# Scan step: the exponent of a power split over two exponentials, log(1 - e) ahead of sg, and seven unread products a step

## The chip, the cores and the metric

The kernel runs on one core of a Trainium2 chip. The metric is the time on the device in microseconds (us). The engines named below work side by side and meet through semaphores: TensorE (PE, matrix products; PEld are its weight loads), VectorE (DVE, elementwise work and reductions), ScalarE (ACT, functions such as exp and log), GpSimd (POOL) and SyncE (SP, which here issues transfers).

## The reference, cut to what matters

The program is a stack of six sublayers over a state of 2 x 2048 tokens with 256 channels. The change touches only the first one, a recurrent scan over 2048 steps. Its state h holds, for each of 2 batches, 256 channels and 16 modes, a complex number (two floats). One step is:

```
h_carrier = h.mean(axis=1)                      # over the 256 channels
T     = cos((phase(xr_t) - phase(h_carrier)) / 2) ** 2
alpha = exp(dt_t * A_neg)
expo  = 1 + (1 - alpha) * 0.5 * (1 - T)
cmag  = min(exp(expo * log(mag(h) + 1e-8)), 10)
h = from_polar(cmag, phase(h)) + B_t * (dt_t * x_t)
h = from_polar(tanh(mag(h)), phase(h))
y_t = sum(C_t * h)
```

Each step needs the h of the step before, and the mean over the channels couples all of them.

## The kernel before, in words

**Layout.** The 2 batches, 16 modes and 4 groups of channels make 128 rows (partitions); the 64 channels of a group lie along the free axis (J = 64). So nearly every operation of a step works on a tile of 128 x 64 floats, and the two parts of a complex number are two such tiles (`p[:, 0]`, `p[:, 1]`).

**Loops.** A hardware loop runs 4 turns of 512 steps; in a turn the steps are unrolled as 32 groups of 16. `step` writes one step. The order of the instructions on each engine is the order in which they are written (`manual_schedule`), each engine runs its own in order, and a semaphore holds an instruction until what it reads is there.

**A step.** hs holds each row's sum of h over its 64 channels, made by the reduction that also writes the new h (hist, L479).

1. PE multiplies hs with a fixed matrix (L408), eight small products into hc and hd, which sum the four groups of channels: the carrier. It then makes the output products of the step before (yps, L490).
2. ACT takes the log of x (lh, L412), squares and sums hc (sq, L416), and gets the inverse length of the carrier by a log and an exponential (L425, ci L426). VectorE forms the dot product of carrier and input direction (dot, L418).
3. The power's exponent less 1, applied to the log of the squared magnitude, is (alpha - 1)/8 times the carrier's cosine less 1. VectorE makes kd and lg, the log of the squared magnitude (L422, L423), and gl = lg times the decay ng (L435). ACT makes ek = exp(kd) (L427), c1 = ci times dot minus 1 (L428, named c in the trace: trailing digits of names are left out there) and fac = exp(c1 times gl) (L440).
4. VectorE multiplies h with ek (L437, L438), then with fac (L443), adds the input bx (L445), and forms the squared magnitudes m2 and r1 (L447 to L454). While it does, ACT prepares the next step's bx (L389) and, in some steps, decays of the next group.
5. ACT takes logs and exponentials: lm, lr, m, ir, e = exp(-2m), rm, le = log(1 + e) (L468, in the trace under m, whose buffer it uses), sg = exp(-le) (L469), then lb, k1, k2c (L471 to L473). tanh(m) is (1 - e) times sg.
6. VectorE multiplies p with ir (L475), with e - 1 (L477), and with -sg in the reduction that writes hist and hs (L479). Behind it stand x, dl and kc for the next step (L483 to L485).

A small product of ci (L431) writes one element of hd; it makes PE wait for ACT and VectorE at that point.

## Time and profile before

| what | us |
|---|---|
| median of 3 runs | 14357.04 (14350.03 to 14368.9) |
| the profiled execution | 14364.49 |
| its span, first to last instruction | 14362.8 |
| busy in the span: DVE, ACT, PE | 9934.6, 9106.3, 5808.5 |
| mean duration of sg, fac, c, lh | 0.223, 0.348, 0.285, 0.256 |
| mean duration of a product into hc, into hd | 0.203, 0.193 |

A line of the timeline gives the start, the duration, the engine, the line of the kernel, the operation, what it writes and reads, its shape and how many instructions it merges; in square brackets stands how long the engine had been idle and what released it. PEclk is TensorE's granted clock as a share of full speed; in the row of slices it is in tenths. Two instructions of one engine overlap in part, so that the spacing of their starts is shorter than a duration.

### The profile page before, as it was taken

To read this page: it belongs to the slowest core of one execution; us is meant where nothing else is said; L and a number is where in the kernel's file an instruction comes from. 1 tells how busy PE (TensorE), PEld (TensorE's weight loads), DVE (VectorE), ACT (ScalarE), POOL (GpSimd) and SP (SyncE) were. 2 spreads that over 40 slices of the span, in tenths; PEclk is the share of its full clock that TensorE was granted. 3 is DMA by queue.
4 is the path that set the end of the run, shared out by engine and by line. 5 is a ranking of instruction groups with operands and counts; after the bars stand their busy time and mean duration, and the time that the engine had idled before them with its cause. 6 is when DMAs were issued, how large, how long until landed. Compare 5 with 4: busy or idle time off the path is not lost. (4 is left out here: it accounts for less than half of the span.)

```text
span 14362.8 us, 279683 instructions
## 1 busy us (share of the span) xinstructions
PE 5808.5 (40%) x76520; PEld 3905.5 (27%) x76520; DVE 9934.6 (69%) x61067; ACT 9106.3 (63%) x46835; POOL 418.8 (3%) x496
## 2 busy tenths in 40 slices
PE   4222222222222222222222222222598665978889
PEld 1111111111111111111111111111355444544445
DVE  6888888788888878888887888888566211455552
ACT  3777877777777777777777777777454100134442
POOL 0000000000000000000000000000000000121110
PEclk6555555555555555555555555555598787989999
DMA  3000000000000000000000000000000677132210
GB/s 78 13 16 15 15 16 16 14 16 16 13 16 16 13 16 16 13 16 16 13 16 16 13 16 16 13 16 16 13 4 14 170 186 174 39 79 35 34 28 14
DMA packets 349068, 460.94 MB, mean 32 GB/s; under 512 B 204930, under 2 KB 244937, under 8 KB 346452
## 3 DMA queue, kind: packets, MB, share of 16 engines
q1 hardware_dynamic: 296276, 319.90, 9.8%
q10 hardware_dynamic: 36352, 88.61, 2.6%
q0 software_dynamic: 14848, 34.36, 0.8%
q8 instruction: 612, 10.03, 0.3%
q14 instruction: 980, 8.03, 0.2%
HBM read 385.55 MB, written 52.46 MB: 30 GB/s over the span
## 5 line engine op out<-in xcount | busy, mean ns | idle before, releaser
L408 PE MATMUL hc<-hs,mean 128*32 128x2 f32 x16384 | 586.3, 203 | 7250.6 <-DVE hs L479 7186.2
L408 PEld LDWEIGHTS hc<-hs,mean 128*32 128x32 f32 x16384 | 410.5, 140 | 7462.8 <-DVE hs L479 7398.0
L475 DVE TENSOR_TENSOR p<-p,ir 128x64 f32<-128x64 f32 x4096 | 739.5, 222 | 1062.4 <-ACT ir L464 1062.4
L490 PE MATMUL yps<-cs,hist 128*64 128x8 f32 x8192 | 1225.0, 259 | 13.4 <-DVE hs L479 13.4
L460 ACT ACTIVATE lm<-m 128x64 f32<-128x64 f32 x2048 | 466.2, 228 | 1179.7 <-DVE m L452 1179.7
L389 ACT ACTIVATE bx<-dx,tc 128x64 f32<-128x64 f32 x4098 | 1169.7, 332 | 0.0
L1519 ACT ACTIVATE d_p<-ps_e 128x512 f32<-128x512 f32 (+3 forms) x1280 | 599.4, 537 | 755.9 <-PE ps_o L1500 537.2
L490 PEld LDWEIGHTS yps<-cs,hist 128*64 128x64 f32 x8192 | 1033.2, 218 | 45.4 <-DVE hs L479 13.8
L443 DVE TENSOR_TENSOR p<-p,fac 128x64 f32<-128x64 f32 x4096 | 739.4, 222 | 421.6 <-ACT fac L440 421.6
L412 ACT ACTIVATE lh<-x 128x64 f32<-128x64 f32 x2048 | 525.2, 256 | 551.1 <-DVE x L483 551.0
L479 DVE CUSTOM_DVE_ANT_0 hist<-p,sg 128x64 f32<-128x64 f32 x4096 | 764.0, 223 | 23.5 <-ACT lb L471 5.1
L440 ACT ACTIVATE fac<-gl,c 128x64 f32<-128x64 f32 x2048 | 712.3, 348 | 68.9 <-DVE p L437 3.0
L477 DVE SCALAR_TENSOR_TENSOR p<-e,p 128x64 f32<-128x64 f32 x4096 | 738.8, 222 | 11.8 <-ACT sg L469 10.5
L445 DVE TENSOR_TENSOR p<-p,bx 128x64 f32<-128x64 f32 x4096 | 723.9, 218 | 0.0
L428 ACT ACTIVATE c<-ci,dot 128x1 f32<-128x1 f32 x2048 | 584.2, 285 | 0.0
L1512 PE MATMUL ps_e<-d_qt,d_kt 128*128 128x512 f32 (+3 forms) x1280 | 556.7, 444 | 43.9 <-ACT d_p L1519 35.5
L1166 PE MATMUL ps_c<-toep,c_x 64*32 64x128 f32 x18432 | 386.0, 321 | 383.8 <-issue 382.7
L1469 PE MATMUL ps_m<-d_kt,d_qt 128*128 128x512 f32 (+3 forms) x1280 | 501.3, 438 | 97.4 <-DVE d_part L1474 37.6
L408 PE MATMUL hd<-hs,mean 128*32 128x2 f32 x16384 | 539.7, 193 | 0.0
L431 PE MATMUL hd<-ident,ci 128*1 128x1 f32 x4096 | 386.9, 164 | 358.8 <-ACT ci L426 358.8
L1479 DVE TENSOR_REDUCE d_part<-ps_m 128x1 f32<-128x512 f32 x768 | 494.7, 683 | 41.7 <-PE ps_m L1469 41.1
L437 DVE SCALAR_TENSOR_TENSOR p<-hist,ek 128x64 f32<-128x64 f32 x2048 | 460.8, 225 | 84.5 <-ACT ek L427 0.9
(441 smaller groups left out, 21583.2 us busy)
## 6 DMA issues: line engine op xcount, KB each, us to landing
toep<-in_C_krev ACTq DMA_DIRECT2D x64, 1216.0 KB, 14.4
toep<-in_C_krev SPq DMA_DIRECT2D x64, 1216.0 KB, 10.1
ng<-dtd SPq DMA_DIRECT2D x258, 256.0 KB, 3.5
dx<-dxd SPq DMA_DIRECT2D x258, 256.0 KB, 4.1
d_kt<-d_kd SPq DMA_DIRECT2D x128, 128.0 KB, 4.3
d_qt<-d_qd SPq DMA_DIRECT2D x128, 128.0 KB, 4.2
y<-ys SPq DMA_DIRECT2D x512, 8.0 KB, 1.9
c_xd<-c_xs POOLq DMA_DIRECT2D x32, 256.0 KB, 6.7
```

The source lines that it names most:

```text
L389: A.activation(bx[o][:, k2], tg[j][2][:, k], AF.Identity, scale=tg[j][0][:, k2, k : k + 1], bias=0.0 if k2 else SMALL,)
L408: nc.tensor.matmul(out[r : r + 32], mean[:, r : r + 32], hs[i], start=True, stop=True)
L428: A.activation(c1, ci, AF.Identity, scale=dot, bias=-1.0)
L440: A.activation(fac, gl, AF.Exp, scale=c1)
L443: V.tensor_tensor(p[:, k2], p[:, k2], fac, ALU.mult)
L445: V.tensor_tensor(p[:, k2], p[:, k2], bx[o][:, k2], ALU.add)
L475: V.tensor_tensor(p[:, k2], p[:, k2], ir, ALU.mult)
L477: V.scalar_tensor_tensor(p[:, k2], e, -1.0, p[:, k2], ALU.add, ALU.mult)
L479: V.tensor_tensor_reduce(out=hn[:, k2], in0=p[:, k2], in1=sg, scale=-1.0, scalar=0.0 if k2 else J * SMALL, op0=ALU.mult, op1=ALU.add, accu ...
L490: nc.tensor.matmul(yps[:, k, :], hist[g][:, k, k2], tg[g][3][:, k2, k], start=k2 == 0, stop=k2 == 1)
L1512: nc.tensor.matmul(s[:, q0:], ks[kt // 4][:, hh, kt % 4 * P : (kt % 4 + 1) * P], q[:, hh, q0:], start=True, stop=not diag,)
L1519: A.activation(pr[:, q0:], s[:, q0:], AF.Exp, scale=0.25)
```

## The change

**The exponent.** With L = lg and gl = L times ng, the old step formed exp(kd) times exp(gl (ci dot - 1)). The new one forms ex = kd - gl and ngd = gl times dot on VectorE, then ea = exp(ex) and fac = exp(ci times ngd) on ACT. c1 is gone.

**Where the logs come from.** x and its log lh are gone. A new log ld = log(1 - e) is taken on ACT right after le and ahead of sg; th = ld - le is the log of the tanh. lg and kd are now made at the end of a step, behind the reduction, from th, kc and dl, and gl at the head of the next, ahead of the dot product. dl is made from p ahead of the reduction, no longer from hist behind it.

**Buffers.** lb uses the buffer of lr in PSUM; its own is gone.

**Seven products.** After the product of ci, PE makes seven products of a 128 x 128 by a 128 x 512 tile of ones in bf16 into a PSUM tile named idle, which nothing reads.

In the setup the same start values are formed with other names, and one tile of ones is written. The core of the diff:

```diff
--- before.py
+++ after.py
@@ -329,7 +329,7 @@
 
             hist = [new(cp, [P, TG, 2, J], f"hist{j}") for j in range(2)]
             hs = [new(cp, [P, 2], f"hs{j}") for j in range(2)]
-            x, kc, dl = ([new(cp, [P, J], f"{n}{j}") for j in range(2)] for n in ("x", "kc", "dl"))
+            lg, kd = ([new(cp, [P, J], f"{n}{j}") for j in range(2)] for n in ("lg", "kd"))
             bx = [new(cp, [P, 2, J], f"bx{j}") for j in range(2)]
             tg = [[new(cp, sh, f"{n}{j}") for n, sh in (
                 ("tc", [P, 6, TG]), ("ng", [P, TG, J]), ("dx", [P, TG, J]),
...
@@ -392,6 +391,8 @@
                 )
 
             hc, hd = new(pp, [P, 2], "hc"), new(pp, [P, 2], "hd")
+            warm, idle = cp.tile([P, 512], BF16, name="warm", tag="warm"), new(pp, [P, 512], "idle")
+            V.memset(warm, 1.0)
             w = lambda sh, name: new(wp, [P, *sh], name)
             wa = lambda name: new(pa, [P, J], name)
 
@@ -408,8 +409,8 @@
                         nc.tensor.matmul(out[r : r + 32], mean[:, r : r + 32], hs[i], start=True, stop=True)
                 before()
 
-                lh, lg, kd = (w([J], n) for n in ("lh", "lg", "kd"))
-                A.activation(lh, x[i], AF.Ln, scale=-1.0)
+                gl, ex, ea, ngd = (w([J], n) for n in ("gl", "ex", "ea", "ngd"))
+                V.tensor_tensor(gl, lg[i], ng, ALU.mult)
 
 
                 sq, n2c = w([2], "sq"), w([1], "n2c")
@@ -419,25 +420,25 @@
                     out=junk, in0=hd, in1=tc_[:, 4:6, k], scale=1.0, scalar=0.0, op0=ALU.mult, op1=ALU.add,
                     accum_out=dot,
                 )
-                V.scalar_tensor_tensor(kd, kc[i], 0.5, dl[i], ALU.mult, ALU.add)
-                V.scalar_tensor_tensor(lg, lh, 2.0, kc[i], ALU.mult, ALU.add)
-                ln, ci, c1, ek = wa("lr")[:, 0:1], w([1], "ci"), w([1], "c1"), w([J], "ek")
+                V.tensor_tensor(ex, kd[i], gl, ALU.subtract)
+                V.tensor_scalar(ngd, gl, dot, None, ALU.mult)
+                ln, ci = wa("lr")[:, 0:1], w([1], "ci")
                 A.activation(ln, n2c, AF.Ln, bias=1e-18)
                 A.activation(ci, ln, AF.Exp, scale=-0.5)
-                A.activation(ek, kd, AF.Exp)
-                A.activation(c1, ci, AF.Identity, scale=dot, bias=-1.0)
+                A.activation(ea, ex, AF.Exp)
 
 
                 nc.tensor.matmul(hd[32:33, 0:1], ci, self.ident[:, 0:1], start=True, stop=True)
 
-
-                gl = w([J], "gl")
-                V.tensor_tensor(gl, lg, ng, ALU.mult)
+                for _ in range(7):
+                    nc.tensor.matmul(idle, warm[:, 0:P], warm, start=True, stop=True)
+
+
                 p = w([2, J], "p")
-                V.scalar_tensor_tensor(p[:, 0], h[:, 0], SMALL, ek, ALU.add, ALU.mult)
-                V.tensor_tensor(p[:, 1], h[:, 1], ek, ALU.mult)
+                V.scalar_tensor_tensor(p[:, 0], h[:, 0], SMALL, ea, ALU.add, ALU.mult)
+                V.tensor_tensor(p[:, 1], h[:, 1], ea, ALU.mult)
                 fac = w([J], "fac")
-                A.activation(fac, gl, AF.Exp, scale=c1)
+                A.activation(fac, ngd, AF.Exp, scale=ci)
                 act_gap(k)
                 for k2 in range(2):
                     V.tensor_tensor(p[:, k2], p[:, k2], fac, ALU.mult)
@@ -460,14 +461,15 @@
                 A.activation(lm, m2, AF.Ln)
                 A.activation(lr, r1, AF.Ln)
                 A.activation(m, lm, AF.Exp, scale=0.5)
-                ir, e, sg, rm = (w([J], n) for n in ("ir", "e", "sg", "rm"))
+                ir, e, sg, rm, ld = (w([J], n) for n in ("ir", "e", "sg", "rm", "ld"))
                 A.activation(ir, lr, AF.Exp, scale=-0.5)
                 A.activation(e, m, AF.Exp, scale=-2.0)
                 A.activation(rm, lm, AF.Exp, scale=-1.0)
                 le = wa("m")
                 A.activation(le, e, AF.Ln, bias=1.0)
+                A.activation(ld, e, AF.Ln, scale=-1.0, bias=1.0)
                 A.activation(sg, le, AF.Exp, scale=-1.0)
-                lb, k1, k2c = wa("lb"), w([J], "k1"), w([J], "k2c")
+                lb, k1, k2c = wa("lr"), w([J], "k1"), w([J], "k2c")
                 A.activation(lb, m2, AF.Ln, bias=MAG_EPS)
                 A.activation(k1, rm, AF.Ln, scale=MAG_EPS, bias=1.0)
                 A.activation(k2c, lb, AF.Exp, scale=-0.5)
@@ -475,14 +477,18 @@
                     V.tensor_tensor(p[:, k2], p[:, k2], ir, ALU.mult)
                 for k2 in range(2):
                     V.scalar_tensor_tensor(p[:, k2], e, -1.0, p[:, k2], ALU.add, ALU.mult)
+                th, kc, dl = (w([J], n) for n in ("th", "kc", "dl"))
+
+                V.scalar_tensor_tensor(dl, p[:, 0], 0.5 * SMALL, rm, ALU.mult, ALU.mult)
                 for k2 in range(2):
                     V.tensor_tensor_reduce(
                         out=hn[:, k2], in0=p[:, k2], in1=sg, scale=-1.0, scalar=0.0 if k2 else J * SMALL,
                         op0=ALU.mult, op1=ALU.add, accum_out=hs[o][:, k2 : k2 + 1],
                     )
-                V.scalar_tensor_tensor(x[o], e, -1.0, sg, ALU.add, ALU.mult)
-                V.scalar_tensor_tensor(dl[o], hn[:, 0], -SMALL, rm, ALU.mult, ALU.mult)
-                V.scalar_tensor_tensor(kc[o], k2c, 2.0 * MAG_EPS, k1, ALU.mult, ALU.add)
+                V.tensor_tensor(th, ld, le, ALU.subtract)
+                V.scalar_tensor_tensor(kc, k2c, 2.0 * MAG_EPS, k1, ALU.mult, ALU.add)
+                V.scalar_tensor_tensor(lg[o], th, 2.0, kc, ALU.mult, ALU.add)
+                V.scalar_tensor_tensor(kd[o], kc, 0.5, dl, ALU.mult, ALU.add)
 
             def project(g, k, yps):
 
```

More of the change, by code (lines that the diff above doesn't have):

```diff
@@ L341, in scan @@
             V.tensor_scalar(hs[1][:, 0:1], hs[1][:, 0:1], J * SMALL, None, ALU.add)
-            n0 = new(wp, [P, J], "lh")
+            n0, n1, n2h = (new(wp, [P, J], n) for n in ("kc", "dl", "th"))
             A.preload_act_table_set(LOG_EXP)
             V.tensor_tensor(n0, first[:, 1], first[:, 1], ALU.mult)
-            V.tensor_tensor(kc[1], first[:, 0], first[:, 0], ALU.mult)
-            V.tensor_tensor(n0, n0, kc[1], ALU.add)
-            A.activation(kc[1], n0, AF.Ln, bias=MAG_EPS)
-            A.activation(x[1], kc[1], AF.Exp, scale=-0.5)
-            V.scalar_tensor_tensor(kc[1], x[1], 2.0 * MAG_EPS, kc[1], ALU.mult, ALU.add)
-            A.activation(n0, n0, AF.Ln)
-            V.tensor_tensor(kc[1], kc[1], n0, ALU.subtract)
-            A.activation(x[1], n0, AF.Exp, scale=-1.0)
-            V.scalar_tensor_tensor(dl[1], first[:, 0], -SMALL, x[1], ALU.mult, ALU.mult)
-            A.activation(x[1], n0, AF.Exp, scale=0.5)
-            V.tensor_scalar(x[1], x[1], -1.0, None, ALU.mult)
+            V.tensor_tensor(n1, first[:, 0], first[:, 0], ALU.mult)
+            V.tensor_tensor(n0, n0, n1, ALU.add)
+            A.activation(lg[1], n0, AF.Ln, bias=MAG_EPS)
+            A.activation(n1, lg[1], AF.Exp, scale=-0.5)
+            V.scalar_tensor_tensor(lg[1], n1, 2.0 * MAG_EPS, lg[1], ALU.mult, ALU.add)
+            A.activation(n0, n0, AF.Ln)
+            V.tensor_tensor(n2h, lg[1], n0, ALU.subtract)
+            A.activation(n1, n0, AF.Exp, scale=-1.0)
+            V.scalar_tensor_tensor(n1, first[:, 0], -SMALL, n1, ALU.mult, ALU.mult)
+            V.scalar_tensor_tensor(kd[1], n2h, 0.5, n1, ALU.mult, ALU.add)
             yv = y.rearrange("p k (b t) -> p k b t", b=B)
```

## The prediction

> **What bounds the kernel now.** I read the slices of the span first. Twenty-eight of forty look alike, with the TensorE clock at 0.5: this is the recurrent scan, 2048 steps one after another.

> ```profile
> span 14362.8 us, 279683 instructions
> DVE  6888888788888878888887888888566211455552
> ACT  3777877777777777777777777777454100134442
> PEclk6555555555555555555555555555598787989999
> ```

> No engine is full in these slices, so the bound is a chain that runs through all the engines. Between 1000.4 and 10183.9 us lie 1915 steps, so a step takes 4.797 us on average and the 2048 take 9824 us, 68% of the span. Next I laid 80 steps of the timeline (5000 to 5400 us) over each other: 71 of them last 4.76 or 4.77 us (4.765 below), the offsets inside agree within 0.01 us, and a few steps are 0.12 to 0.35 us longer. One such step, start first, then duration:

> ```profile
> 5004.30 0.22 DVE L483 SCALAR_TENSOR_TENSOR x<-e,sg 128x64 f32<-128x64 f32 x1
> 5004.44 0.29 PE L408 MATMUL hc<-hs,mean 128*32 128x2 f32 x8 [3.83 <-DVE hs L479]
> 5004.80 0.17 ACT L416 ACTIVATE sq<-hc 128x2 f32<-128x2 f32 x1
> 5004.90 0.16 DVE L418 CUSTOM_DVE_ANT_0 junk<-hd,tc 128x2 f32<-128x2 f32 x1
> 5005.13 0.22 DVE L423 SCALAR_TENSOR_TENSOR lg<-lh,kc 128x64 f32<-128x64 f32 x1
> 5005.30 0.17 ACT L426 ACTIVATE ci<-lr 128x1 f32<-128x1 f32 x1
> 5005.38 0.22 DVE L435 TENSOR_TENSOR gl<-lg,ng 128x64 f32<-128x64 f32 x1
> 5005.51 0.28 ACT L428 ACTIVATE c<-ci,dot 128x1 f32<-128x1 f32 x1
> 5005.83 0.35 ACT L440 ACTIVATE fac<-gl,c 128x64 f32<-128x64 f32 x1
> 5006.21 0.36 DVE L443 TENSOR_TENSOR p<-p,fac 128x64 f32<-128x64 f32 x2 [0.20 <-ACT fac L440]
> 5008.07 0.36 DVE L475 TENSOR_TENSOR p<-p,ir 128x64 f32<-128x64 f32 x2 [0.56 <-ACT ir L464]
> 5008.19 0.23 ACT L468 ACTIVATE m<-e 128x64 f32<-128x64 f32 x1
> 5008.40 0.36 DVE L477 SCALAR_TENSOR_TENSOR p<-e,p 128x64 f32<-128x64 f32 x2
> 5008.45 0.22 ACT L469 ACTIVATE sg<-m 128x64 f32<-128x64 f32 x1
> 5008.77 0.23 DVE L479 CUSTOM_DVE_ANT_0 hist<-p,sg 128x64 f32<-128x64 f32 x1
> ```

> Take T as the start of x (5004.30). The reader should see one ring: the sums hs, the mean products on PE (T+0.14), sq, ci (T+1.00), c, fac (T+1.52), then VectorE's p times fac (T+1.90), a middle part, and hist (T+4.47), which is 0.30 before the next T. Gaps tell where time goes: c takes 0.28 and fac waits for it.

> **Spacings used**, all from these steps. Independent VectorE operations start 0.14 apart. A dependent one starts 0.26 after its source (lg to gl). ACT to VectorE or back costs 0.03 after the end (ek ends T+1.31, p starts T+1.34). An operation that waits for two engines starts 0.19 after its predecessor in a pair, 0.33 after the pair's first (L475 to L477). A reduction starts about 0.15 after an ordinary operation: in the attention stage at 13641.24 and 13641.85 it follows a reduce 0.61 later, where two reduces stand 0.595 apart. Logarithm to the next ACT operation: 0.15 (k1 to k2c).

> **Part 1, the first half of a step (T to p times fac).** Removed are lh (0.26 on ACT, beside PE's work, so worth nothing: sq starts 0.07 after PE is done with hc) and c (0.28, on the path). What takes c's place as the last thing is VectorE's new chain, which now precedes the exponentials. In the order in which the changed kernel issues it:
> - th T+0, kc T+0.14, lg (needs kc) T+0.40, kd T+0.54, gl (needs lg) T+0.67, the dot product T+0.82 with its accumulator read T+0.91;
> - ex (needs gl) T+0.93, ngd (needs dot) T+1.07, ended T+1.29;
> - ea on ACT at ex's end: 0.93 + 0.22 + 0.03 = T+1.18, ended T+1.43 (0.25, as ek);
> - the pair p from ea T+1.46 and T+1.60, and p times fac, a two-engine wait on that pair, at 1.46 + 0.33 = T+1.79;
> - fac itself: not before ea + 0.15 = T+1.33, nor before ngd's end with about 0.03 to 0.11 for its two waits, T+1.32 to T+1.40; with 0.35 + 0.03 it releases VectorE at T+1.71 to T+1.78, just earlier.

> So p times fac moves from T+1.90 to T+1.79: **-0.11 us a step**. The bounds are -0.16 (fewer wait penalties) and -0.05 (fac's waits cost more).

> **Part 2, the second half.** Two operations enter ahead of hist. ld, a logarithm, goes on ACT behind le: before, sg waited 0.26 after le began, for its result, and ld takes 0.15 of that. sg then starts at 3.88 + 0.15 + 0.15 = T+4.18 rather than 4.14, and is ready at T+4.43. On VectorE dl stands behind the L477 pair (T+4.10, 4.24). It waits for both engines, so it starts at 4.10 + 0.33 = T+4.43. hist follows at 4.43 + 0.15 = T+4.58 instead of 4.47: **+0.11 us a step**. Bounds: +0.04 if dl starts 0.14 after its pair and hist 0.14 after dl, +0.19 if hist keeps the 0.23 distance it has now from the operation ahead of it. sg, ready 0.15 before, hides ld; without that cover ld would cost up to 0.15. lb, k1 and k2c slip by 0.04; k2c is ready near T+4.85, kc asks for it at 4.58 + 0.30 + 0.14 = T+5.02. lb's move into lr's buffer adds no wait: users of both run in order on ACT.

> [...] le, with that bias, lasts 0.23 and k1 0.25, and k2c starts 0.15 after k1. I take the rows.

> **Part 3, seven products.** bf16 128x128 by 128x512, behind the ci product (T+1.22 to 1.41). No such product is in the trace. The nearest row is a 512-column product of attention at the slow clock: L1469 at 13389.17, the next at 13389.60, so 0.43 each with its weight load hidden. 7 x 0.43 = 3.0: they end near T+4.45 and PE is next wanted at T+4.77+0.14. They cost nothing; the cover is 0.4 us a step. At 0.53 each (a 0.10 load, as of L983's bf16 weights, exposed) they would end at T+5.1 and delay the sums by 0.2.

> Do they raise the clock, and does that help? [...] after 10300 us, 1189 consecutive stretches of 3.413 us each show a clock of exactly 0.5 or 1. For instance (span, PE busy, PE weight loads, VectorE, ACT, POOL, clock):

> ```profile
> 11235.57:11238.99 3.41, 3.41 (x128) 3.00 (x114) 0.00 (x0) 0.00 (x0) 0.00 (x0) 0.50 0.59 149
> 11238.99:11242.40 3.41, 2.24 (x98) 1.94 (x101) 0.66 (x2) 1.07 (x2) 0.00 (x0) 1.00 0.12 25
> 11245.81:11249.23 3.41, 0.24 (x18) 0.00 (x0) 0.00 (x0) 0.00 (x0) 0.00 (x0) 1.00 1.07 260
> 11249.23:11252.64 3.41, 0.47 (x23) 0.47 (x30) 0.00 (x0) 0.00 (x0) 0.00 (x0) 0.50 1.09 258
> ```

> A full stretch is followed by clock 1, a stretch that is 7% busy by 0.5. All 104 rises follow at least 0.76 busy; most of 103 falls less than 0.4. The new step has PE busy some 90% while slow and 55% when fast, so the clock should go up and fall back at times: a mean of 0.6 to 0.95, I take 0.8. [...] By the rows they release nothing: at the slow clock ci would already let fac start at T+1.21 and dot's input is there at T+0.60, while VectorE asks for them at T+1.33 and T+0.82. So 0, with -0.02 a step as the other end.

> **Sum.** -0.11 + 0.11 + 0 = 0.00 us a step, with ends of about -0.12 and +0.14 if all lean one way. Two more VectorE operations a step lengthen the occasional long steps (0.03 a step now) by 2/26, +0.002, 5 us in all; the setup's changed lines are a handful of operations. Against the profiled execution (span 14362.8, 14364.5 in all) that gives 14370; the median of the runs is 7.4 lower, so 14362 on its scale.

> **Rivals.**
> - *Slower, by dl ahead of hist* (36%). hist is held 0.165 to 0.19 rather than 0.11 if the reduction again keeps the 0.23 after the operation ahead of it. It decides once hist stands 0.14 or more after its old offset with the first half as forecast; at 0.19 the step loses 0.08, +164 us: 14526. For it: hist stands 0.23 behind L477 today. Against: there hist itself has two waits, after the change one.
> - *Faster* (29%). dl doesn't wait its second wait out, hist moves only 0.04: net -0.07, -143 us: 14219. Or the faster clock counts because VectorE's chain is quicker than summed. Against: the L475 to L477 pair has exactly dl's form and shows 0.33.
> - *Products in the way* (inside the slower case, 3%): above 0.5 us each they push the mean products; at 0.53 and a slow clock +0.2 x 2048 = +410 us. For it: the weights are loaded seven times. Against: the 0.43 row.
> - *The products don't lift the clock*: PEclk stays 0.5 in the scan, time as forecast, since PE isn't on the path either way.

> **How the numbers follow.** Two tenths of a percent (29 us, 0.014 a step) is about what a measurement of this kernel can tell from no change. No change within it: 35%, the likeliest, 14362, own range 14333 to 14391. Faster 29%, slower 36%. Halving the ends of the rivals gives roughly -0.05 and +0.055 a step as what leaves out a tenth on each side: 14255 to 14475.

> **What would show it.** p times fac at T+1.79 (right if 1.75 to 1.83), ea starting at T+1.18 on ex, hist at T+4.58 with dl 0.15 ahead, sg not the last to arrive; period 4.75 to 4.79. Wrong if fac is released by ci (then PE counts), if mean products wait for PE's queue, or if hist starts with sg's end.

## The result and the profile after

The changed kernel takes 14329.0 us (median of 20 runs) where the kernel before takes 14351.7 us in the same runs: ratio 0.9985, 95% interval 0.9979 to 0.9991. That is 22.7 us less, 0.15%: inside the band of 0.2% that the prediction called no change, but with 20 runs a side it is resolved. It is a small gain where exactly none was forecast. The profiled execution of the changed kernel was the longest of its 20 (14342.7 us, span 14341.0).

The page of the changed kernel, its head and slices:

```profile
span 14341.0 us, 310403 instructions
...
DVE  6888888888888888888888888888576111455552
ACT  3777777777777777777777777777354000134442
...
PEclk6777776777777777777777777777698787989999
```

The scan still fills the same slices and neither VectorE nor ACT is full. TensorE's clock in the scan went from 0.50 to 0.72 on average; the time barely moved. Whether the faster clock bought any of the small gain, the first experiment tests.

One step from the timeline (start, duration, engine, line); T is the start of th:

```profile
5051.51 0.22 DVE L488 TENSOR_TENSOR th<-ld,m 128x64 f32<-128x64 f32 x1
5051.65 0.29 PE L409 MATMUL hc<-hs,mean 128*32 128x2 f32 x8 [0.95 <-DVE hs L484]
5051.90 0.22 DVE L490 SCALAR_TENSOR_TENSOR lg<-th,kc 128x64 f32<-128x64 f32 x1
5052.00 0.17 ACT L417 ACTIVATE sq<-hc 128x2 f32<-128x2 f32 x1 [0.55 <-PE hc L409]
5052.18 0.22 DVE L413 TENSOR_TENSOR gl<-lg,ng 128x64 f32<-128x64 f32 x1
5052.43 0.23 DVE L423 TENSOR_TENSOR ex<-kd,gl 128x64 f32<-128x64 f32 x1
5052.50 0.17 ACT L427 ACTIVATE ci<-lr 128x1 f32<-128x1 f32 x1
5052.69 0.26 ACT L428 ACTIVATE ea<-ex 128x64 f32<-128x64 f32 x1
5052.85 2.96 PE L434 MATMUL idle<-warm 128*128 128x512 bf16 x7
5052.91 0.35 ACT L441 ACTIVATE fac<-ngd,ci 128x64 f32<-128x64 f32 x1
5052.98 0.23 DVE L438 SCALAR_TENSOR_TENSOR p<-hist,ea 128x64 f32<-128x64 f32 x1 [0.16 <-ACT ea L428]
5053.31 0.36 DVE L444 TENSOR_TENSOR p<-p,fac 128x64 f32<-128x64 f32 x2
5055.45 0.24 ACT L470 ACTIVATE ld<-e 128x64 f32<-128x64 f32 x1
5055.50 0.36 DVE L479 SCALAR_TENSOR_TENSOR p<-e,p 128x64 f32<-128x64 f32 x2
5055.59 0.20 ACT L471 ACTIVATE sg<-m 128x64 f32<-128x64 f32 x1
5055.83 0.23 DVE L482 SCALAR_TENSOR_TENSOR dl<-p,rm 128x64 f32<-128x64 f32 x1
5055.97 0.22 DVE L484 CUSTOM_DVE_ANT_0 hist<-p,sg 128x64 f32<-128x64 f32 x1
```

ea starts as soon as ex is there (T+1.18), 0.02 after ci has ended, and p times fac starts at T+1.80 behind the pair p. The rows of the two pages for p times fac, before and after, show the same: VectorE's idle time ahead of it, 421.6 us that ended with fac, has shrunk to 9.8 us.

```profile
L443 DVE TENSOR_TENSOR p<-p,fac 128x64 f32<-128x64 f32 x4096 | 739.4, 222 | 421.6 <-ACT fac L440 421.6
L444 DVE TENSOR_TENSOR p<-p,fac 128x64 f32<-128x64 f32 x4096 | 741.3, 222 | 9.8 <-DVE p L444 6.2
```

In the second half sg has ended at 5055.79, 0.18 before hist starts: hist stands behind dl. The timeline prints hundredths of a microsecond, which is too coarse here; the records of the trace have nanoseconds. With the short steps between 5000 and 5400 us laid over each other (72 before, 69 after), the offsets are these (medians, in us). sq stands at 0.49 in the step shown, whose mean products are slow (0.29), and at 0.447 in most.

| from T, us | before | forecast | after |
|---|---|---|---|
| sq | 0.495 | 0.49 | 0.447 |
| ea | (ek 1.062) | 1.18 | 1.171 |
| fac | 1.526 | 1.33 to 1.40 | 1.398 |
| p times fac | 1.906 | 1.79 | 1.789 |
| from p times fac to the e - 1 pair | 2.194 | as before | 2.194 |
| from that pair to hist | 0.369 | 0.48 | 0.471 |
| from hist to the next T | 0.297 | 0.30 | 0.290 |
| a short step | 4.766 | 4.765 | 4.744 |

So 0.117 us is gained in the first half, 0.102 is lost between the pair and hist, and 0.007 is gained behind hist. The net -0.022 is worth -45 us over 2048 steps. Part is given back by steps that are longer than the short ones: over the scan, with the gaps of some 12 us between the four turns of the loop left out, they add 39 us before and 52 us after, 0.019 and 0.026 us a step. With the gaps 2 us shorter this gives -45 + 13 - 2 = -34 us, and in the two profiled executions the scan, from the first T to the last, is indeed 33.7 us shorter (9819.6 to 9785.9).

These two executions as a whole differ by 21.8 us only, since the rest of the program, nearly all of it behind the scan, took 11.9 us longer. The change does not touch the program behind the scan, and there the ten traces of this case range from 4159 to 4184 us. Whether the change has a share in these 12 us, one trace a kernel can't say.

### The profile page after: what moved, and what is told of

Read it like the earlier page. It is cut to its first block, busy times and chain, and to the rows that moved or that the text cites. A ratio compares the mean times of both kernels' runs of the same rounds, so it can differ in the third digit from the quotient of the medians.

```text
span 14341.0 us, 310403 instructions
## 1 busy us (share of the span) xinstructions
PE 10559.7 (74%) x90856; PEld 5123.5 (36%) x90856; DVE 10322.3 (72%) x65164; ACT 8537.4 (60%) x44786; POOL 419.0 (3%) x496
## 5 line engine op out<-in xcount | busy, mean ns | idle before, releaser
L434 PE MATMUL idle<-warm 128*128 128x512 bf16 x14336 | 5241.6, 528 | 0.0
L434 PEld LDWEIGHTS <-warm 128*128 128x128 bf16 x14336 | 1567.3, 121 | 2187.0 <-issue 1601.2
L409 PE MATMUL hc<-hs,mean 128*32 128x2 f32 x16384 | 533.0, 190 | 2182.5 <-DVE hs L484 2117.9
L409 PEld LDWEIGHTS hc<-hs,mean 128*32 128x32 f32 x16384 | 356.8, 120 | 3741.8 <-DVE hs L484 3676.7
L477 DVE TENSOR_TENSOR p<-p,ir 128x64 f32<-128x64 f32 x4096 | 738.0, 221 | 1062.4 <-ACT ir L465 1062.4
L417 ACT ACTIVATE sq<-hc 128x2 f32<-128x2 f32 x2048 | 352.4, 172 | 1107.9 <-PE hd L409 672.4
L496 PE MATMUL yps<-cs,hist 128*64 128x8 f32 x8192 | 969.4, 227 | 2.5 <-DVE hs L484 2.5
L496 PEld LDWEIGHTS yps<-cs,hist 128*64 128x64 f32 x8192 | 780.5, 167 | 38.2 <-DVE hs L484 5.7
L479 DVE SCALAR_TENSOR_TENSOR p<-e,p 128x64 f32<-128x64 f32 x4096 | 739.8, 221 | 5.4 <-DVE p L479 4.1
L441 ACT ACTIVATE fac<-ngd,ci 128x64 f32<-128x64 f32 x2048 | 712.2, 348 | 1.0 <-DVE p L438 1.0
L438 DVE SCALAR_TENSOR_TENSOR p<-hist,ea 128x64 f32<-128x64 f32 x2048 | 460.1, 225 | 322.5 <-ACT ea L428 322.4
L428 ACT ACTIVATE ea<-ex 128x64 f32<-128x64 f32 x2048 | 524.3, 256 | 81.0 <-DVE ex L423 4.9
```

Source lines behind the costliest of these rows:

```text
L409: nc.tensor.matmul(out[r : r + 32], mean[:, r : r + 32], hs[i], start=True, stop=True)
L434: nc.tensor.matmul(idle, warm[:, 0:P], warm, start=True, stop=True)
L441: A.activation(fac, ngd, AF.Exp, scale=ci)
L477: V.tensor_tensor(p[:, k2], p[:, k2], ir, ALU.mult)
L479: V.scalar_tensor_tensor(p[:, k2], e, -1.0, p[:, k2], ALU.add, ALU.mult)
L496: nc.tensor.matmul(yps[:, k, :], hist[g][:, k, k2], tg[g][3][:, k2, k], start=k2 == 0, stop=k2 == 1)
```

## The experiments

The theory: the first half is held by VectorE's chain kc, lg, gl, ex, then ea and p, so that PE's clock releases nothing; the second half is held by dl alone, and ld hides behind the wait of sg. The rivals: the clock is what brought the gain, and ld holds hist. Ratios are to the kernel before, with 95% intervals.

### The changed kernel without the seven products

```diff
-                for _ in range(7):
-                    nc.tensor.matmul(idle, warm[:, 0:P], warm, start=True, stop=True)
```

> The changed kernel without the seven unread products; everything else as in it. Theory (VectorE's chain kc, lg, gl, ex, ea, p holds the first half, so the products release nothing): the clock falls back to 0.50 in the scan, sq starts 0.04 us later than in the changed kernel (T+0.49 instead of T+0.45), p times fac stays at T+1.79, the short step stays at 4.74 us; the long steps may get fewer[...]: 14329 or up to 15 us less. Rival (the faster clock is what made the changed kernel's step 0.02 us shorter): the step grows by 0.02 to 0.04 us, 14370 to 14410.

Measured: 14342.2 us, ratio 0.9987 (0.9981 to 0.9994). Both kernels took some 10 us more in these runs than in those of the result (before 14361.9), so the ratios are what can be compared. The clock is back at 0.5. One step:

```profile
5052.69 0.22 DVE L484 TENSOR_TENSOR th<-ld,m 128x64 f32<-128x64 f32 x1
5053.18 0.17 ACT L415 ACTIVATE sq<-hc 128x2 f32<-128x2 f32 x1 [0.55 <-PE hc L407]
5054.48 0.36 DVE L440 TENSOR_TENSOR p<-p,fac 128x64 f32<-128x64 f32 x2
```

sq is back at T+0.49, and p times fac stays at T+1.79; the short step is 4.747 against 4.744, where the rival asked for 0.02 to 0.04 more. The ratio is within 0.0002 of that of the full change (0.9985), with intervals of 0.0006 to each side: if the products give or cost anything in this kernel, it is not more than about 12 us (an estimate from the two intervals). Their absence did not take the long steps away (they add 58 us in the scan, against 52 with the products), so the products are not what makes them, which I had thought possible.

### The seven products alone, in the kernel before

```diff
+                for _ in range(7):
+                    nc.tensor.matmul(idle, warm[:, 0:P], warm, start=True, stop=True)
...
-                lb, k1, k2c = wa("lb"), w([J], "k1"), w([J], "k2c")
+                lb, k1, k2c = wa("lr"), w([J], "k1"), w([J], "k2c")
```

> The kernel before with the seven products alone (lb shares lr's buffer, as in the change, to make room). In this kernel sq, ci, c and fac are the ring, so a PE that is done earlier should count: sq moves from T+0.49 to T+0.45 on average at a clock near 0.77, p times fac from T+1.90 to T+1.86, the step from 4.765 to 4.725 us: -82 us, less some 15 us for more long steps, so about 14285. Rival (PE is off the path here as well, or the products cost as much as they give): within 0.2% of before.

Measured: 14310.5 us, 0.9961 (0.9947 to 0.9975): -51 us. The sign is as the theory has it, the size smaller. The reason is in the timeline of this kernel:

```profile
5044.43 0.22 DVE L488 SCALAR_TENSOR_TENSOR x<-e,sg 128x64 f32<-128x64 f32 x1
5044.57 0.24 PE L410 MATMUL hc<-hs,mean 128*32 128x2 f32 x8 [1.88 <-DVE hs L484]
5046.30 0.36 DVE L448 TENSOR_TENSOR p<-p,fac 128x64 f32<-128x64 f32 x2 [0.21 <-ACT fac L445]
5049.15 0.22 DVE L488 SCALAR_TENSOR_TENSOR x<-e,sg 128x64 f32<-128x64 f32 x1
5049.29 0.28 PE L410 MATMUL hc<-hs,mean 128*32 128x2 f32 x8 [0.85 <-DVE hs L484]
5051.06 0.36 DVE L448 TENSOR_TENSOR p<-p,fac 128x64 f32<-128x64 f32 x2 [0.20 <-ACT fac L445]
5053.92 0.22 DVE L488 SCALAR_TENSOR_TENSOR x<-e,sg 128x64 f32<-128x64 f32 x1
```

The two steps are of two kinds. In the first the eight products into hc take 0.24, p times fac starts 1.87 after x, and the step lasts 4.72. In the second they take 0.28, it starts at 1.91, and the step lasts 4.77, as in the kernel before; so lb's shared buffer, which this run has as well, costs nothing. A fast clock at the mean products is worth 0.043 us a step, and over the scan 1142 of 1894 short steps have it: 0.043 x 0.60 x 2048 = 53 us. I had reckoned as if every step gained. The same products that buy 51 us in the kernel before buy nothing that could be measured in the changed one: the change took PE off the ring.

### dl moved out of the way of the reduction

```diff
-                V.scalar_tensor_tensor(dl, p[:, 0], 0.5 * SMALL, rm, ALU.mult, ALU.mult)
...
                 V.scalar_tensor_tensor(kc, k2c, 2.0 * MAG_EPS, k1, ALU.mult, ALU.add)
+                V.scalar_tensor_tensor(dl, p[:, 0], 0.5 * SMALL, rm, ALU.mult, ALU.mult)
                 V.scalar_tensor_tensor(lg[o], th, 2.0, kc, ALU.mult, ALU.add)
```

> The changed kernel with dl moved from ahead of the reduction into the gap between kc and lg, where lg waits for kc anyway. Theory (dl is all that holds hist up): hist stands 0.37 us behind the first e - 1 product again instead of 0.47, T+4.35 for T+4.45, the step falls by 0.10 to 4.64 us, -205 us: about 14125. Rival (ld ahead of sg holds hist as much as dl does): hist waits for sg, which is ready at T+4.31, with its two waits at T+4.39 to 4.42: the step falls by 0.03 to 0.06 only, 14205 to 14270.

Measured: 14173.3 us, 0.9864 (0.9849 to 0.9879), -189 us to before. Its timeline, VectorE and sg of one step:

```profile
5056.50 0.36 DVE L479 SCALAR_TENSOR_TENSOR p<-e,p 128x64 f32<-128x64 f32 x2
5056.60 0.20 ACT L471 ACTIVATE sg<-m 128x64 f32<-128x64 f32 x1
5056.87 0.23 DVE L483 CUSTOM_DVE_ANT_0 hist<-p,sg 128x64 f32<-128x64 f32 x1
...
5057.30 0.22 DVE L488 SCALAR_TENSOR_TENSOR kc<-k2c,k 128x64 f32<-128x64 f32 x1
5057.44 0.22 DVE L489 SCALAR_TENSOR_TENSOR dl<-p,rm 128x64 f32<-128x64 f32 x1
5057.57 0.22 DVE L490 SCALAR_TENSOR_TENSOR lg<-th,kc 128x64 f32<-128x64 f32 x1
```

hist stands 0.37 behind the pair's first again, as in the kernel before, where the changed kernel has 0.47. By the rival it would be 0.41 to 0.44. The step is 4.667, not 4.64. lg now starts 0.270 after kc where it had 0.251, which puts p times fac at T+1.805 instead of 1.789, so dl is not wholly free in the gap; and what was gained behind hist, 0.007, is gone again.

### dl moved, and no products

> The changed kernel with dl between kc and lg and without the seven products. By the theory that the products release nothing: the same short step as with dl moved and the products kept, and up to 15 us less for fewer long steps. By the rival that the clock counts: 0.02 to 0.04 us a step, 40 to 80 us, more than with the products.

Measured: 14173.4 us, 0.9868 (0.9853 to 0.9883), at a clock of 0.5 in the scan. It equals the run above; with and without products the mean step between 1000 and 4000 us is 4.707 us. This is the simplest of the kernels here that beat both, by 188 us to before.

### ld behind sg

```diff
                 A.activation(le, e, AF.Ln, bias=1.0)
-                A.activation(ld, e, AF.Ln, scale=-1.0, bias=1.0)
                 A.activation(sg, le, AF.Exp, scale=-1.0)
+                A.activation(ld, e, AF.Ln, scale=-1.0, bias=1.0)
```

> The changed kernel with ld behind sg instead of ahead of it; dl stays ahead of the reduction. Theory (sg isn't what hist waits for, dl is): sg starts 0.04 us earlier, T+4.04, and hist stays at T+4.45; step 4.74 us, 14340 on the scale where before has 14362, that is the changed kernel's own time within 15 us. Rival (ld ahead of sg costs its 0.15): hist earlier by up to 0.15, the step 4.60 to 4.70, 80 us or more off.

Measured: 14344.6 us, 0.9984 (0.9977 to 0.9990). The two ends of one step:

```profile
5053.15 0.22 DVE L488 TENSOR_TENSOR th<-ld,m 128x64 f32<-128x64 f32 x1
...
5057.18 0.23 ACT L470 ACTIVATE sg<-m 128x64 f32<-128x64 f32 x1
5057.47 0.23 DVE L482 SCALAR_TENSOR_TENSOR dl<-p,rm 128x64 f32<-128x64 f32 x1
5057.61 0.22 DVE L484 CUSTOM_DVE_ANT_0 hist<-p,sg 128x64 f32<-128x64 f32 x1
```

sg starts at T+4.03 instead of 4.08, hist stays at T+4.46. ld ahead of sg costs nothing as long as dl stands where it does.

### Both behind

> The changed kernel with dl between kc and lg and ld behind sg. Theory: hist is set by the 0.37 us behind the first e - 1 product, not by sg, so no gain over dl alone moved (4.67 us, 14173); and ld in the way of k2c may make kc late: k2c is then ready near T+4.80, kc asks for it at T+4.67 + 0.13 = 4.80, so 0 to +0.05 us a step, 14173 to 14275. Rival (sg holds hist once dl is out of the way): hist 0.04 earlier, 14090.

Measured: 14277.3 us, 0.9937 (0.9923 to 0.9950): 90 us less than before, where dl alone moved gave 189 less, so about 100 us of that is lost, at the unfavourable end of the theory. One step:

```profile
5051.01 0.36 DVE L479 SCALAR_TENSOR_TENSOR p<-e,p 128x64 f32<-128x64 f32 x2
5051.06 0.23 ACT L470 ACTIVATE sg<-m 128x64 f32<-128x64 f32 x1
5051.38 0.23 DVE L483 CUSTOM_DVE_ANT_0 hist<-p,sg 128x64 f32<-128x64 f32 x1
...
5051.61 0.21 ACT L475 ACTIVATE k2c<-lr 128x64 f32<-128x64 f32 x1
5051.68 0.22 DVE L487 TENSOR_TENSOR th<-ld,m 128x64 f32<-128x64 f32 x1
5051.86 0.23 DVE L488 SCALAR_TENSOR_TENSOR kc<-k2c,k 128x64 f32<-128x64 f32 x1
```

hist keeps its 0.37 to the pair, although sg starts 0.05 behind that pair here and 0.10 in the run with dl alone moved; so an earlier sg releases nothing. But ld has pushed k2c: it ends at 5051.82, and kc starts 0.18 after th instead of 0.13. Everything behind kc is late by that, and the short step is 4.72 instead of 4.67. With dl moved, ld ahead of sg, in sg's own waiting time, is the better place, against the look of it.

### Twelve products instead of seven

In the changed kernel, and alone in the kernel before:

```diff
-                for _ in range(7):
+                for _ in range(12):
```

> The changed kernel with twelve unread products a step instead of seven. At the slow clock they last 12 x 0.427 = 5.1 us, longer than a step, so that they would hold the mean products; at the fast clock 12 x 0.213 = 2.6 us, done by T+3.9. Theory: PE's stretches are now full, the clock stays at 1 nearly always, and since PE releases nothing, the step stays at 4.74 us: within 20 us of the changed kernel, at a mean clock in the scan above 0.95. Rival (the clock still falls back often): each fall costs a step of some 1.5 us more, which at one fall in ten steps is +300 us.

> The kernel before with twelve unread products a step (lb shares lr's buffer). With seven its short steps were of two kinds, 4.72 and 4.76 us, and the clock 0.77. Theory (the gain comes from the clock at the mean products): at a clock near 1 all short steps are of the first kind, so 0.045 us a step under before, -90 us: 14270 where before has 14362. Rivals: the products' own load on the queue gives it away again (14310 or more), or the clock falls back and steps are held (above 14362).

Measured: in the changed kernel 14425.9 us, 1.0040 (1.0026 to 1.0054); alone in the kernel before 14335.7 us, 0.9980 (0.9972 to 0.9988). The clock is 0.97 and 0.99 on average (between 2600 and 4000 us), so both theories had the short step right: 4.75 and 4.72 us. What they underrated is the fall of the clock. In the changed kernel's timeline with twelve:

```profile
5052.83 4.13 PE L434 MATMUL idle<-warm 128*128 128x512 bf16 x11 [0.16 <-issue]
5056.05 0.22 DVE L488 TENSOR_TENSOR th<-ld,m 128x64 f32<-128x64 f32 x1
5056.89 0.28 PE L409 MATMUL hc<-hs,mean 128*32 128x2 f32 x8
...
5061.38 0.22 DVE L488 TENSOR_TENSOR th<-ld,m 128x64 f32<-128x64 f32 x1
```

The granted clock fell to 0.5 for 3.4 us inside the products, whose weight loads stand 0.43 apart in this timeline from 5053.77 to 5055.90; at another such fall in this trace, 2729.09 to 2732.51, the mean clock is 0.51. They lasted 4.13 us where those of the steps around it took 2.5 to 2.8, the mean products start 0.84 after th instead of 0.14, and the step lasts 5.33. In the changed kernel with twelve, 141 of the 2047 steps are held in this way, by 0.59 us on average: +83 us, for +79 measured against the change itself (1.0040 to 0.9985). In the kernel before with twelve the short step gains 0.043 (-88 us), and 77 held steps take 61 us of it back, by 0.79 us each: -27 us, for -32 measured (before 14367.3 in these runs). This is the rival of the products in the way, at twelve; at seven no step shows it.

## Why the prediction was right or wrong

- **First half, -0.11 us a step: right in its mechanism, 0.007 short.** Each start of the chain kc, lg, gl, ex, ea, p is within 0.02 us of the forecast, p times fac within 0.001. What was off is the old offset: 1.906 where the sum took 1.90 (its own row gives 1.91). VectorE's chain, and not fac or ci, was the last to arrive, as read; but fac was not far behind. In the kernel before, p times fac waited for fac and followed its end by 0.032; now it follows by 0.043, so fac had only 0.01 to spare.
- **Second half: mis-sized, and with it the sum.** The failed step is "hist follows at 4.43 + 0.15 = T+4.58 instead of 4.47: +0.11 us a step", which the sum sets against -0.11 to get 0.00. It measures +0.102: dl came 0.329 behind the pair's first, as forecast, but hist followed dl by 0.142 where I took 0.15, a spacing from another stage. The sum also kept the 0.30 from hist to the next T; it went from 0.297 to 0.290. That 0.007 lies between the two reductions, and it goes with hist's place: 0.144 apart in every trace where dl stands ahead of hist, 0.151 where hist follows the pair itself.
- **Why so small a miss counts.** The three misses are 0.007 to 0.008 each, less than the 0.01 to which the rows were read. They happen to have the same sign and add up to -0.022 a step, -45 us. The mechanism held; the 0.00 in the middle was not a result but the difference of two nearly equal numbers, each rounded: 0.02 us on it is 41 us in 2048 steps, more than the band that was called no change.
- **ld at nothing: right** (ld behind sg changes nothing while dl stands ahead of hist). In the changed kernel ld starts 0.162 behind le and sg 0.146 behind ld, 0.308 from le to sg where the kernel before has 0.259. sg stands at T+4.08 with ld ahead of it and at T+4.03 with ld behind it, so ld put it back by 0.04 to 0.05, as the rows said.
- **Products at nothing: right** within what was measured, shown by leaving them out. They take 2.96 at the slow clock, as forecast (3.0), and hold no step; in the changed kernel's trace most of them start 0.427 apart at the slow clock and 0.216 at the fast one. The mean clock was forecast at 0.8; between 2600 and 5000 us it is 0.72.
- **Long steps, +0.002: too low.** They grew by 0.006. In all six traces of the changed scan with seven products or none, wherever dl and ld stand, they add 50 to 58 us, and 39 in the kernel before; held steps apart, they add 52 and 35 us with twelve products. That they come with the two added VectorE operations fits this, but no run shows it; what stalls VectorE in them the profile does not name.
- **The faster rival** had a right place, hist behind dl, but not this mechanism: dl's two waits were paid in full (it starts 0.329 behind the pair's first), and the faster clock did not count (p times fac at T+1.79 with the products and without). **The slower rival** did not occur: the reduction, now with one wait, follows at 0.142.

## What to carry to other kernels

In a recurrence, count what a change adds between the last partial result and the value that the next step waits for: here one operation ahead of the reduction took back 0.102 of the 0.117 us a step that the shorter exponent gave, and moving it into a gap where its engine waited anyway made 0.15% into 1.3%. Raising TensorE's clock paid here only where a small product was on the ring (51 us in the kernel before, nothing that could be measured in the changed one), and then only in the steps whose products met the fast clock (0.043 us each). When a forecast is the difference of two terms of the same size, read both as finely as the trace allows, and give the difference the width of their rounding times the number of steps.
